# Turning the context rows of six batches and one gated tile by transposing transfers instead of TensorE, in a fused attention and FP4 feed-forward kernel

## The chip, the cores and the metric

The kernel runs on one core of one Trainium2 chip. Its time is the device time of one execution in microseconds (us); several executions give a median. One further execution is recorded by the hardware profiler: its rows give every instruction with start and duration, its "span" runs from the first to the last instruction. The engines are named as the profile names them: PE is TensorE (PEld its weight loads), DVE is VectorE, ACT is ScalarE, POOL is GpSimd and SP is SyncE, which issues all DMA transfers of this kernel. All arithmetic is in 32-bit floats.

## The reference, cut to what matters

There are 8 batches (B) of x, 512 rows (S) of 256 values (D), and for each batch 64 context rows z. For every batch:

```python
y0 = layernorm(x)
r  = layernorm(y0 + softmax(causal(y0 @ y0.T / 16)) @ y0) * g1 + beta1
r  = layernorm(r + softmax(r @ z.T / 16) @ z) * g2 + beta2           # cross attention
r  = layernorm(r + relu(r @ w1 + b1) @ w2 + b2) * g3 + beta3         # MLP, 1024 wide
x  = x + r
q  = fp4(layernorm(x))                                               # blocks of 16 along the row
h  = silu(q @ fp4(w_gate).T) * (q @ fp4(w_up).T)                     # 704 wide
x  = x + fp4(h) @ fp4(w_down).T
```

`fp4` scales each block of 16 by its largest magnitude and rounds to eight magnitudes and a sign. Every product contracts over the last dimension of both operands or over rows, so many tiles are needed transposed, with the contracted dimension on the 128 partitions.

## The kernel before

Each batch is five stages: 0 load and self attention, 1 cross attention, 2 MLP, 3 quantization of the normed x and the gate and up products, 4 quantization of h and the down product. The 512 rows are four tiles of 128 (NT = 4), D is two chunks of 128 (ND = 2). The MLP is 64 products a batch at L985 (512 columns wide, eight hidden chunks) and L1005; the gate and up products stand at L1060, the down product at L1140 (six chunks for each of four tiles).

**Order.** Nothing is issued as the code is read. Every function records operations in a `Plan`: engine, modelled cost, tiles read and written. `Plan._keys` gives each operation a key, the latest start by which it would meet its batch's and stage's entry in the table `DUE`: a due reaches back through all successors, and within a batch from each PE operation to the one before it, so the smallest due of a later stage decides. `push` is added to the keys of the weights' preparation, of fills and of loads. `Plan.order` then plays a list schedule with modelled costs, transfer delays (`lag`) and tile homes: a free engine takes the ready operation with the smallest key, if a home is free for each tile that it first uses. The list that results is emitted once, and each engine and SP's queue follow it strictly in order; semaphores make an instruction wait for its inputs. So `DUE`, the `push` values, and the numbers of homes (`plan.kind`, `plan.share`) set the order, and an instruction that waits holds up all behind it on its engine.

**Two ways to transpose.** `transposed` (L419) lets PE transpose blocks against the identity into a PSUM bank (L427), and ACT copies the bank to SBUF. `turned_by_transfers` (L861) has ACT copy the tile so that the low and the high 16-bit halves of the 32-bit values lie apart (L867), writes it to DRAM (L873), and reads it back by a 16-bit transposing transfer (L878) that lays the halves side by side again. Which way y0, r and r again go is set by `BY_PRODUCTS` (4, 2, 1): PE does it for y0 of the first four batches, for r in cross attention of the first two, and for r in the MLP of the first. The quantized x (`zqT`) always goes by transfers.

**z.** `load` (L351) puts the 64 rows of z twice into a 128-partition tile (`z`, L368), with columns of ones from a fill. `cross_attention` (L884) turns z by PE for every batch: two transposes of 64x128, and ACT writes `zT` with the factor 1/16 (L891). `zT` is the stationary operand of the key products at L907, from which ACT copies `kq` (L920), PE transposes it (L924) and so on to the values product at L951, which reads z itself.

**The down product.** `down` (L1086) quantizes h and makes `hqT`. For all batches but the last: ACT sets the halves apart (L1095), SP writes `hd` (L1101) and issues the transposing transfer (L1106). For the four tiles of the last batch `turned_by_products` (L1116) transposes six blocks on PE, four at L427 and two at L1126, and ACT evicts them in three copies (L1119, L1129, L1130). `last` (L1135) does the product at L1140, the addition to x on DVE (L1151) and the write of the result (L1158). In the last batch all four gate and up tiles are recorded ahead of the four down tiles.

Of the kernel before, what the change touches and what calls it, by code (L numbers as in the profile page):

```python
# [12 lines left out]
U16 = mybir.dt.uint16  # L13
AF = mybir.ActivationFunctionType
# [5 lines left out]
P = 128  # L20
# [18 lines left out]
TURN = 2.6  # L39
# [2 lines left out]

TILED = 2.65

BY_PRODUCTS = (4, 2, 1)
LOAD_EARLY = 2121.0
DUE = [
    [-1946.0, 1210.0, 1271.0, -94.0, 168.0],
    [-339.0, 1223.0, -124.0, -48.0, 115.0],
    [-106.0, 818.0, -121.0, 513.0, 497.0],  # L50
    [2633.0, 342.0, -95.0, 819.0, 286.0],
    [1411.0, 380.0, 1328.0, 1549.0, 28.0],
    [594.0, -260.0, -745.0, -950.0, 427.0],
    [741.0, -2228.0, 778.0, 530.0, 88.0],
    [812.0, 363.0, 145.0, 267.0, -1093.0],
    [-2273.0],
]


# [8 lines left out]
def act(cols, bias=False):  # L68
    return 0.06 + cols * 0.84e-3 + 0.19 * bias
# [193 lines left out]
def kernel(  # L263
# [19 lines left out]
    nc = tc.nc  # L283

    B, S, D = x.shape
    SZ = z.shape[1]
    DFF = w1.shape[1]
    I = w_gate.shape[0]
    NT = S // P
    ND = D // P  # L290
    NF = DFF // P
    NI = -(-I // P)
# [7 lines left out]
    dram = ctx.enter_context(tc.tile_pool(name="dram", bufs=1, space=DRAM))  # L300
# [6 lines left out]
    def several(name, count, shape):  # L307
        return [fixed(f"{name}_{k}", shape) for k in range(count)]


    plan = Plan(due=DUE)
# [1 line left out]

    y0_homes = several("y0", 2, [P, NT, D + 2])

    z_homes = several("z", 8, [P, D + 2])
    plan.kind("y0", y0_homes)
    plan.kind("z", z_homes)
    plan.kind("zT", several("zT", 6, [P, ND, SZ]))
    plan.kind("turned", several("turned", 3, [P, ND, S]), ordered=False)  # L320
    plan.share("y0T", "turned", 3)
    plan.share("yT", "turned", 3, ordered=False)
    plan.share("zqT", "turned", 3)
    plan.kind("e", several("e", 1, [P, NT * (NT + 1) // 2 * P]))
    plan.kind("r", several("r", 3, [P, NT, D]))
    plan.kind("kq", several("kq", 4, [P, S // 2]))
    plan.kind("xp", several("xp", 1, [P, NT, SZ]))
    plan.kind("xpT", several("xpT", 7, [P, NT // 2 * P]))
    plan.kind("hT", several("hT", 9, [P, S]))
    plan.kind("zq", several("zq", 1, [P, NT, D]))  # L330
    plan.kind("zm", several("zm", 2, [P, NT * D]), ordered=False)
    plan.kind("wide", several("h", 8, [P, NI * P]), ordered=False)
    plan.share("h", "wide", 5)
    plan.share("hm", "wide", 4)
    plan.share("wq", "wide", 5)
    hqT_homes = several("hqT", 3, [P, NI * P])
    plan.kind("hqT", hqT_homes)

    hd_homes = [dram.tile([P, 2, NI * P], U16, tag=f"hd_{k}", name=f"hd_{k}") for k in range(3)]
# [3 lines left out]
    zd_homes = [dram.tile([NT, P, 2, D], U16, tag=f"zd_{k}", name=f"zd_{k}") for k in range(4)]  # L343
    plan.kind("zd", zd_homes, ordered=False)
    plan.kind("ln", several("ln", 13, [P, 48]), ordered=False)
    plan.kind("q", several("q", 6, [P, 3, 64]), ordered=False)
    plan.kind("rt", several("rt", 7, [P, 4]), ordered=False)
    banks = [psum.tile([P, 512], F32, tag=f"bank{k}", name=f"bank_{k}") for k in range(8)]
    plan.kind("bank", banks, ordered=False)
# [511 lines left out]
    def turned_by_transfers(v, view, m, yT):  # L861
# [19 lines left out]
            reads=[d], writes=[(yT, c) for c in range(ND)], lag=TURN,  # L881
        )

    def cross_attention(b, r, zs):  # L884

        plan.stage = 1
        zT = plan.buf("zT")
        transposed(
            lambda: [zs.ap[:SZ, ts(c, P)] for c in range(ND)], [(zs, 0)], (zT, None),

            lambda pt: nc.scalar.activation(  # L891
                zT.ap, pt[:, : ND * SZ].rearrange("p (c k) -> p c k", c=ND),
                AF.Copy, scale=1.0 / 16.0,
            ),
            act(ND * SZ), 2,
        )
        yT = turned(r, "yT", b < BY_PRODUCTS[1], lambda t: r.ap[:, t, :])
        sc, nm, xp = plan.buf("bank"), plan.buf("rt"), plan.buf("xp")

        keys = plan.buf("bank")

        def products():
            for c in range(ND):
                for i in range(2):
                    nc.tensor.matmul(  # L907
                        keys.ap[ts(i, SZ), : S // 2], zT.ap[:, c, :], yT.ap[:, c, ts(i, S // 2)],
                        start=(c == 0), stop=(c == ND - 1),
                    )  # L910

        def exps():
            for t in range(NT):
                nc.scalar.activation(
                    xp.ap[:, t, :], sc.ap[:, ts(t, SZ)], AF.Exp, bias=nm.ap[:, t : t + 1]
                )

        plan.op("PE", 1.05, products, reads=[yT, zT], writes=[keys])
        kq = plan.buf("kq")
        plan.op("ACT", act(S // 2), lambda: nc.scalar.copy(kq.ap, keys.ap[:, : S // 2]), reads=[keys], writes=[kq])  # L920

        def scores():
            for j in range(2):
                nc.tensor.transpose(sc.ap[:, ts(j, P)], kq.ap[:, ts(j, P)], ident)  # L924

        plan.op("PE", 0.24, scores, reads=[kq], writes=[sc])
        plan.op(
            "DVE", 0.36,
            lambda: nc.vector.tensor_reduce(
                nm.ap, sc.ap[:, : NT * SZ].rearrange("p (t k) -> p t k", k=SZ),  # L930
                AX.X, ALU.max, negate=True,
            ),
            reads=[sc], writes=[nm],
        )
        plan.op("ACT", 0.8, exps, reads=[sc, nm], writes=[xp], table="exp")
        xpT = plan.buf("xpT")
        transposed(
            lambda: [
                xp.ap[:, 2 * j : 2 * j + 2, :].rearrange("p t k -> p (t k)") for j in range(NT // 2)
            ],  # L940
            [xp], (xpT, None), lambda pt: nc.scalar.copy(xpT.ap, pt[:, : NT // 2 * P]),
            act(NT // 2 * P), NT // 2,
        )
        s = plan.buf("ln")
        avs = [plan.buf("bank") for _ in range(NT)]


        def values():
            for k in range(NT):
                half = ts(k % 2, SZ)  # L950
                nc.tensor.matmul(  # L951
                    avs[k // 2 + NT // 2 * (k % 2)].ap[:, : D + 2], xpT.ap[half, ts(k // 2, P)],
                    zs.ap[half, :],
                    start=True, stop=True,
                )

        plan.op("PE", TILED * pe(D + 2), values, reads=[xpT, zs], writes=avs)
        for t in range(NT):
            av, rt = avs[t], plan.buf("rt")

# [82 lines left out]
    def glu(b, xs, s):  # L1043
# [5 lines left out]
        zT = plan.buf("zqT")  # L1049
# [36 lines left out]
        def down(t, h):  # L1086
            plan.stage = 4
            m = fp4(h, lambda h=h: h.ap[:, :I], "hm", NBI)
            hqT = plan.buf("hqT")
            if b < B - 1:  # L1090
                hd = plan.buf("hd")
                planes = lambda: m.ap[:, :I].bitcast(U16).rearrange("p (h k) -> p h k", h=2)
                plan.op(
# [4 lines left out]
                    reads=[h], writes=[m],  # L1098
# [61 lines left out]
            )  # L1160


        if b == B - 1:
            hs = [gate_up(t) for t in range(NT)]
            for t in range(NT):
                down(t, hs[t])
        else:
            for t in range(NT):
                down(t, gate_up(t))
# [13 lines left out]

    plan.op("PE", 0.22 * WARM, warm, writes=[idle])
    columns()
    plan.push = 3314.0
    plan.op(
        "POOL", 0.2, lambda: nc.gpsimd.memset(nothing, 0), writes=[(ready["fills"], "nothing")]
    )
# [15 lines left out]
        "SP", 5.2, lambda: nc.sync.dma_start(w2_sb, w2.rearrange("(c p) d -> p c d", p=P)),  # L1205
        writes=[ready["w2"]],
    )
    plan.push = 3314.0
    weights()
    plan.push = 0.0  # L1210
    for b in range(B):
# [38 lines left out]
```

## Time and profile before

| what | value |
|---|---|
| median of three runs | 577.25 us (576.84 to 577.31) |
| profiled execution | 577.01 us |
| its span, first to last instruction | 575.1 us |
| mean granted clock of PE | 0.999 |
| PE busy | 567.1 us, 2231 matmuls |
| DVE busy | 447.3 us |
| ACT busy | 361.2 us |
| transfers by the page | 66.88 MB, mean 116 GB/s |
| PE transposes of z (L427) | 16, 2.2 us busy |
| PE transposes of the last batch's h (L427, L1126) | 16 and 8, 2.4 and 2.2 us busy |

Busy time counts the time in which an engine runs at least one instruction; PE's matmuls overlap one another, so a row's mean length is more than the time it takes out of PE's stream, and the distance from one start to the next is what a run of them costs. In answers that list groups, a row has the start and the length in us, then engine, line, operation, output from input, the count, and in brackets how long the engine had been idle and what released it. In the chain of waits, each piece is the part of the time that one group accounts for on the path to the end.

### The profile page before, as it was taken

How to read it: one execution, taken by the hardware profiler on the slowest of the kernel's cores; microseconds unless marked ns; L12 is line 12 of the kernel's file. 1: busy time of each engine (PE TensorE's matmuls, PEld its weight loads, DVE VectorE, ACT ScalarE, POOL GpSimd, SP SyncE). 2: the span in 40 equal slices, each digit the busy share in tenths (PEclk: the TensorE clock that was granted, in tenths of full speed). 3: DMA queues.
4: the chain of work that ended last, by engine and by line, in shares of the span. 5: the costliest groups of instructions: out<-in, count | busy, mean ns of one | idle time of the engine just before them, and what ended most of it. 6: DMA issues, size and time to landing. Idle time of an engine off the chain costs nothing.

```text
span 575.1 us, 7092 instructions
## 1 busy us (share of the span) xinstructions
PE 567.1 (99%) x2231; PEld 395.7 (69%) x2231; DVE 447.3 (78%) x1128; ACT 361.2 (63%) x758; POOL 63.7 (11%) x93
## 2 busy tenths in 40 slices
PE   8999999999999999999999999999999999999997
PEld 6757584775577668476686666767674867877686
DVE  5889968989397964679479999989898457489892
ACT  2678858697967674676727457959766255455331
POOL 3421101011101200200100001200010000000000
PEclk9999999999999999999999999999999999999999
DMA  8550395273737044054422646893455221645601
GB/s 243 126 192 7 91 228 137 69 203 63 177 99 185 11 90 97 24 133 99 118 46 73 162 124 153 206 200 80 118 158 137 62 62 38 161 108 150 161 18 46
DMA packets 143220, 66.88 MB, mean 116 GB/s; under 512 B 107976, under 2 KB 142672, under 8 KB 143184
## 3 DMA queue, kind: packets, MB, share of 16 engines
q1 hardware_dynamic: 143184, 66.44, 45.3%
q8 instruction: 17, 0.28, 0.2%
q14 instruction: 19, 0.16, 0.1%
HBM read 10.42 MB, written 29.66 MB: 70 GB/s over the span
## 4 chain that ended last, share of the span: by engine, by line
PE 94%; DVE 2%; DMA 1%; ACT 1%; POOL 1%; issue 0%; SPq 0%
PE bank L1060 25%; PE bank L1005 19%; PE bank L985 19%; PE bank L1140 14%; PE bank L818 6%; PE bank L785 5%; PE bank L427 2%; PE bank L951 1%; PE bank L907 1%; DMA turned<-zd 1%; POOL ln L511 1%; DMA x<-in_x_dram 0%; DVE x L574 0%; DVE r L825 0%; ACT squares L496 0%
## 5 line engine op out<-in xcount | busy, mean ns | idle before, releaser
L1060 PE MATMUL bank<-wgu,turned 128*128 128x352 f32 x512 | 157.7, 461 | 0.0
L1060 PEld LDWEIGHTS bank<-wgu,turned 128*128 128x128 f32 x512 | 96.4, 190 | 52.6 <-issue 3.9
L1005 PE MATMUL bank<-w,hT 128*128 128x256 f32 x512 | 113.5, 380 | 0.0
L985 PE MATMUL bank<-turned,w 128*128 128x512 f32 x256 | 112.9, 594 | 0.4 <-DMA turned<-zd 0.4
L1005 PEld LDWEIGHTS bank<-w,hT 128*128 128x128 f32 x512 | 96.8, 190 | 14.1 <-issue 0.4
L985 PEld LDWEIGHTS bank<-turned,w 128*128 128x128 f32 x256 | 48.2, 190 | 56.3 <-issue 50.4
L1140 PE MATMUL bank<-wd,hqT 128*128 128x256 f32 x384 | 86.4, 380 | 0.0
L1140 PEld LDWEIGHTS bank<-wd,hqT 128*128 128x128 f32 x384 | 72.8, 190 | 12.9 <-issue 2.0
L511 POOL TENSOR_TENSOR ln<-ln,mhalf 128x4 f32<-128x4 f32 x32 | 40.4, 1262 | 355.1 <-DVE ln L504 355.1
L620 DVE SCALAR_TENSOR_TENSOR h<-h,h 128x704 f32<-128x704 f32 (+2 forms) x76 | 66.8, 883 | 7.9 <-ACT h L614 7.6
L496 ACT ACTIVATE squares<-r,ln 128x256 f32<-128x256 f32 x96 | 48.7, 507 | 26.7 <-DVE ln L488 24.4
L993 ACT ACTIVATE hT<-bank,cols 128x512 f32<-128x512 f32 x64 | 42.9, 683 | 24.3 <-PE bank L985 24.1
L1072 ACT ACTIVATE h<-bank 128x352 f32<-128x352 f32 x64 | 29.0, 460 | 42.5 <-PE bank L1060 42.2
L1095 ACT COPY h<-h 128x1408 uint16<-128x1408 uint16 x28 | 38.0, 1363 | 19.3 <-DVE h L627 14.9
L614 ACT ACTIVATE h<-h 128x704 f32<-128x704 f32 (+2 forms) x38 | 29.8, 787 | 21.1 <-DVE h L608 16.6
L1079 DVE TENSOR_TENSOR h<-h,bank 128x352 f32<-128x352 f32 x64 | 32.3, 510 | 11.6 <-PE bank L1060 5.2
L785 PE MATMUL bank<-turned 128*128 128x512 f32 (+3 forms) x128 | 38.3, 444 | 0.3 <-ACT turned L853 0.2
L818 PE MATMUL bank<-y,e 128*128 128x258 f32 x160 | 37.0, 383 | 0.4 <-POOL e L805 0.4
L595 DVE TENSOR_REDUCE q<-h 128x44 f32<-128x704 f32 (+2 forms) x38 | 33.2, 878 | 2.9 <-DMA h<-in_L_ffn_w_up_dram 2.8
L818 PEld LDWEIGHTS bank<-y,e 128*128 128x128 f32 x160 | 30.1, 190 | 6.6 <-issue 1.0
L1016 DVE SCALAR_TENSOR_TENSOR r<-bank,r 128x256 f32<-128x256 f32 x32 | 13.4, 421 | 26.9 <-PE bank L1005 26.6
L608 DVE SCALAR_TENSOR_TENSOR h<-h,q 128x704 f32<-128x704 f32 (+2 forms) x38 | 33.4, 884 | 0.2
(94 smaller groups left out, 645.1 us busy)
## 6 DMA issues: line engine op xcount, KB each, us to landing
zd<-zm SPq DMA_DIRECT2D x25, 512.0 KB, 3.1
hd<-h SPq DMA_DIRECT2D x30, 352.0 KB, 3.1
out_dram<-x SPq DMA_DIRECT2D x32, 128.0 KB, 1.7
x<-in_x_dram SPq DMA_DIRECT2D x7, 512.0 KB, 4.9
w<-in_L_xattn_w_dram SPq DMA_DIRECT2D x2, 1024.0 KB, 6.4
z<-in_ctx_dram SPq DMA_DIRECT2D x16, 64.0 KB, 5.2
zd<-h SPq DMA_DIRECT2D x2, 384.0 KB, 4.7
h<-in_L_ffn_w_down_dram SPq DMA_DIRECT2D x2, 352.0 KB, 3.8
```

Of the source, the lines that this page charges most:

```text
L496: lambda t=t: nc.scalar.activation(squares, view(t), AF.Square, bias=s.ap[:, 24 + t : 25 + t], accum_out=s.ap[:, 28 + t : 29 + t],),
L511: lambda: nc.gpsimd.tensor_tensor(s.ap[:, 36:40], s.ap[:, 32:36], mhalf, ALU.pow),
L608: lambda: nc.vector.scalar_tensor_tensor(blocks_of(view()), blocks_of(view()), TIE, each(rc()), ALU.mult, ALU.mult),
L620: lambda reverse=reverse, f=f: nc.vector.scalar_tensor_tensor(view(), mm(), LEAST, view(), ALU.max, f, reverse1=reverse),
L785: nc.tensor.matmul(sc.ap[:, :n], yT.ap[:, c, ts(k, P)], yT.ap[:, c, k * P :], start=(c == 0), stop=(c == ND - 1),)
L818: nc.tensor.matmul(av.ap[:, : D + 2], e.ap[:, ds(start[k] + (t - k) * P, P)], y0.ap[:, k, :], start=(k == 0), stop=(k == t),)
L985: nc.tensor.matmul(hp.ap, w1_sb[:, c, ts(f, P)], yT.ap[:, c, :], start=(c == 0), stop=(c == ND - 1),)
L993: lambda f=f, hp=hp, h=h: nc.scalar.activation(h.ap, hp.ap, AF.Relu, bias=b1_sb[:, f : f + 1]),
L1005: nc.tensor.matmul(fp.ap[:, :D], hT[f].ap[:, ts(t, P)], w2_sb[:, f, :], start=(f == 0), stop=(f == NF - 1),)
L1060: nc.tensor.matmul(gp.ap[:, :HI], zT.ap[:, c, ts(t, P)], wgu[:, c, ds(j * I + n * HI, HI)], start=(c == 0), stop=(c == ND - 1),)
L1095: lambda: nc.scalar.copy(planes(), h.ap[:, :I].bitcast(U16).rearrange("p (k h) -> p h k", h=2)),
L1140: nc.tensor.matmul(op.ap[:, :D], hqT.ap[:, ts(c, P)], wd[:, c, :], start=(c == 0), stop=(c == NI - 1),)
```

## The change

z of batches 0 and 1 is still turned by PE; from batch 2 on the new function `z_by_transfers` does it: a scaled copy of the 64 rows on ACT, a second ACT copy that sets the halves apart, a write to DRAM and a transposing transfer into `zT`, both issued by SP. The last batch's first tile of h (t = 0) goes the way of the other batches' tiles; its other three still go by PE. Homes are added for the new tiles (`zzd` in DRAM, `zpl` in SBUF), and several numbers of homes, the dues, and the pushes of loads, fills and weights are other numbers.

```diff
+Z_BY_PRODUCTS = 2
 BY_PRODUCTS = (4, 2, 1)
-LOAD_EARLY = 2121.0
+LOAD_EARLY = 2211.0
 DUE = [
-    [-1946.0, 1210.0, 1271.0, -94.0, 168.0],
-    [-339.0, 1223.0, -124.0, -48.0, 115.0],
-    [-106.0, 818.0, -121.0, 513.0, 497.0],
-    [2633.0, 342.0, -95.0, 819.0, 286.0],
-    [1411.0, 380.0, 1328.0, 1549.0, 28.0],
-    [594.0, -260.0, -745.0, -950.0, 427.0],
-    [741.0, -2228.0, 778.0, 530.0, 88.0],
-    [812.0, 363.0, 145.0, 267.0, -1093.0],
-    [-2273.0],
+    [-2135.0, 912.0, 1321.0, -107.0, 321.0],
+    [-352.0, 741.0, 238.0, -35.0, 165.0],
+    [164.0, 846.0, -113.0, 420.0, 733.0],
+    [3239.0, 169.0, -88.0, 878.0, 398.0],
+    [879.0, 335.0, 1676.0, 1843.0, 36.0],
+    [598.0, -989.0, -910.0, -604.0, 416.0],
+    [263.0, -2512.0, -326.0, 906.0, -708.0],
+    [-1000.0, -823.0, -1514.0, -1037.0, -2102.0],
+    [-2343.0],
 ]
...
-    z_homes = several("z", 8, [P, D + 2])
+    z_homes = several("z", 7, [P, D + 2])
...
-    plan.share("y0T", "turned", 3)
+    plan.share("y0T", "turned", 1)
...
-    plan.kind("kq", several("kq", 4, [P, S // 2]))
-    plan.kind("xp", several("xp", 1, [P, NT, SZ]))
-    plan.kind("xpT", several("xpT", 7, [P, NT // 2 * P]))
-    plan.kind("hT", several("hT", 9, [P, S]))
+    plan.kind("zzd", [dram.tile([SZ, 2, D], U16, tag=f"zzd_{k}", name=f"zzd_{k}") for k in range(4)])
+    plan.kind("zpl", several("zpl", 4, [SZ, D]))
+    plan.kind("kq", several("kq", 2, [P, S // 2]))
+    plan.kind("xp", several("xp", 3, [P, NT, SZ]))
+    plan.kind("xpT", several("xpT", 8, [P, NT // 2 * P]))
+    plan.kind("hT", several("hT", 8, [P, S]))
...
-    plan.share("hm", "wide", 4)
-    plan.share("wq", "wide", 5)
-    hqT_homes = several("hqT", 3, [P, NI * P])
+    plan.share("hm", "wide", 8)
+    plan.share("wq", "wide", 7)
+    hqT_homes = several("hqT", 4, [P, NI * P])
...
-    plan.kind("q", several("q", 6, [P, 3, 64]), ordered=False)
+    plan.kind("q", several("q", 11, [P, 3, 64]), ordered=False)
...
+    def z_by_transfers(zs, zT):
+        zpl, zd = plan.buf("zpl"), plan.buf("zzd")
+        def apart():
+            nc.scalar.mul(zpl.ap, zs.ap[:SZ, :D], 1.0 / 16.0)
+            nc.scalar.copy(
+                zpl2.ap.bitcast(U16).rearrange("p (h k) -> p h k", h=2),
+                zpl.ap.bitcast(U16).rearrange("p (k h) -> p h k", h=2),
+            )
+        zpl2 = plan.buf("zpl")
+        plan.op("ACT", act(D) + act(2 * D), apart, reads=[(zs, 0)], writes=[zpl, zpl2])
+        plan.op(
+            "SP", 0.5,
+            lambda: nc.sync.dma_start(
+                zd.ap, zpl2.ap.bitcast(U16).rearrange("p (h k) -> p h k", h=2)
+            ),
+            reads=[zpl2], writes=[zd], takes=[zT], lag=1.5,
+        )
+        plan.op(
+            "SP", 0.6,
+            lambda: nc.sync.dma_start_transpose(
+                zT.ap.rearrange("p c k -> p (c k)").bitcast(U16).rearrange(
+                    "p (c r) -> p c r", c=ND
+                ),
+                zd.ap.rearrange("p h k -> (p h) k"),
+            ),
+            reads=[zd], writes=[zT], lag=TURN,
+        )
...
-        transposed(
...
+        if b < Z_BY_PRODUCTS:
+            transposed(
...
+        else:
+            z_by_transfers(zs, zT)
...
-            if b < B - 1:
+            if b < B - 1 or t < 1:
...
-    plan.push = 3314.0
+    plan.push = 4718.0
...
-    plan.push = 3314.0
+    plan.push = 4718.0
```

More of the change, by code (lines that the diff above doesn't have):

```diff
@@ L887, in cross_attention @@
         zT = plan.buf("zT")
-        transposed(
[L889 to L896, printed above, removed]
+        if b < Z_BY_PRODUCTS:
+            transposed(
+                lambda: [zs.ap[:SZ, ts(c, P)] for c in range(ND)], [(zs, 0)], (zT, None),
+                lambda pt: nc.scalar.activation(
+                    zT.ap, pt[:, : ND * SZ].rearrange("p (c k) -> p c k", c=ND),
+                    AF.Copy, scale=1.0 / 16.0,
+                ),
+                act(ND * SZ), 2,
+            )
+        else:
+            z_by_transfers(zs, zT)
         yT = turned(r, "yT", b < BY_PRODUCTS[1], lambda t: r.ap[:, t, :])
```

## The prediction

> **What bounds the kernel now.** I read first the page's busy times, then the table of busy time by stretch, then TensorE (PE) alone in order of time, then the chain that ended last, and at the end the DMA issues. The page:
>
> ```profile
> span 575.1 us, 7092 instructions
> ...
> PE 567.1 (99%) x2231; PEld 395.7 (69%) x2231; DVE 447.3 (78%) x1128; ACT 361.2 (63%) x758; POOL 63.7 (11%) x93
> ```
>
> PE is busy 567.1 of 575.1 us. The profiled execution took 577.01 us, 1.91 us of it outside the span; the median of the three runs is 577.25 us, 0.24 us more. I sum against 577.01. Where the 8.0 idle us lie is told by the stretches (columns: stretch, its length, busy us of each engine, granted clock, DMA share, GB/s):
>
> ```profile
> 0.00:45.00 45.00, 40.89 (x197) 29.40 (x198) 33.79 (x140) 25.34 (x67) 15.91 (x40) 1.00 0.62 179
> 45.00:130.00 85.00, 85.00 (x334) 57.73 (x334) 74.07 (x204) 67.42 (x155) 11.30 (x16) 1.00 0.50 126
> 130.00:300.00 170.00, 169.56 (x645) 114.67 (x644) 120.74 (x317) 113.55 (x247) 16.51 (x18) 1.00 0.39 95
> 300.00:440.00 140.00, 139.68 (x531) 95.38 (x531) 129.78 (x297) 97.74 (x180) 15.66 (x16) 1.00 0.58 146
> 440.00:550.00 110.00, 110.00 (x420) 79.63 (x419) 76.03 (x151) 51.83 (x96) 4.36 (x4) 1.00 0.37 97
> 550.00:575.10 25.10, 21.98 (x112) 18.89 (x110) 12.91 (x24) 5.36 (x15) 0.00 (x0) 0.98 0.11 37
> ```
>
> The reader is to see that from 45 to 550 us PE is idle for 0.44 + 0.32 = 0.76 us in all; 4.11 us are lost before 45 and 3.12 us after 550, nearly all of the latter behind the last matmul. So a PE instruction taken out after 45 us is worth what it occupies, as long as other engines keep feeding. Before 45 us it is worth that only where PE wasn't about to wait anyway.
>
> **Part 1: z of batches 2 to 7.** Two 64-wide transposes for each of six batches go, twelve in all. In the old kernel every z is turned early, before it is needed (L427 in order of time):
>
> ```profile
> 14.69 0.46 PE L427 MATMUL bank<-ident,z 64*128 64x64 f32 x4
> ...
> 32.42 0.34 PE L427 MATMUL bank<-ident,z 64*128 64x64 f32 x2
> ...
> 33.70 0.59 PE L427 MATMUL bank<-ident,z 64*128 64x64 f32 x6
> 35.33 0.44 PE L924 MATMUL bank<-ident,kq 128*128 128x128 f32 x2 [1.05 <-ACT kq L920]
> ...
> 44.04 0.34 PE L427 MATMUL bank<-ident,z 64*128 64x64 f32 x2
> ```
>
> z tiles are taken in order of batch. The first pair (at 6.30 us) is batch 0; the four at 14.69 are batches 1 and 2, then 3, then 4 to 6, then 7. The chain of waits gives the four at 14.69 a share of 0.39 us and the last pair 0.27 us; so one costs about 0.10 to 0.13 us there. On the chain are therefore batch 2's pair, 0.20, and batch 7's, 0.27: **0.47 us**. The eight of batches 3 to 6 lie beside DVE and POOL work, at 8 x 0.105 = 0.84 us; the six at 33.70 are followed by a PE wait of 1.05 us for ACT, so with the order unchanged their removal only lengthens waits. The new order may put other work there: 0 to 0.84 us. I take 0.4, the middle, since the transposes of batch 3's y stand 16 us later in the same list (49.61) and need only a load and a norm.
>
> What replaces them: per batch two ACT instructions, two transfers. ACT: the first is a 64x256 scaled copy, bounded by the 128x256 eviction at L920, 367 ns, and the 128x256 ACT write of y at L541, 595 ns; the second has the form of L867 (512 uint16 columns), 615 ns on 128 rows. Gone is L891, 268 ns. Net 0.71 to 0.94 us a batch, 4.3 to 5.7 us in all, on an engine with 214 us idle. ACT is fullest between 45 and 130 us (67.4 of 85), and 17.6 us are free even there; nothing on the chain, and some 0.9 us for an ACT-fed matmul if the cover is gone.
>
> SP: a write to DRAM and a transpose for each batch. Not in this trace; the nearest rows in both directions:
>
> ```profile
> hqT<-hd SPq DMA_TRANSPOSE x28, 4.0
> turned<-zd SPq DMA_TRANSPOSE x25, 4.3
> ...
> rest_d<-h SPq DMA_DIRECT2D x2, 64.0 KB, 2.8
> ...
> wgu<-rest_d SPq DMA_TRANSPOSE x4, 2.3
> ```
>
> The write is near rest_d (2.8 us to landing); the transpose of 128 x 256 lies between wgu<-rest_d (2.3) and turned<-zd (4.3). Chain of z: 1.0 + 2.8 + 2.3 to 4.3 + the copies' handovers = about 6 to 8.5 us. Consumers are the eight groups of L907: batch 2 at 88.0, then 160.1, 170.9, 220.1, 386.4 and 404.0. z has landed by about 32 us, so 50 us or more cover it; cost nothing, and up to 8.5 us once if the planner issued a z right before its L907. On SP, issue is 0.34 to 0.63 us for the write and 1.1 to 1.4 us for the transpose: 9 to 12 us more in 575 on a queue whose waits already add to hundreds of us. Behind each new wait (the write for ACT, the transpose for the write) stand the yT and hqT transfers; PE's one wait on such a transfer today is 0.44 us (L985 for turned), so I charge 0 and keep 0.4 us for each that meets a tight one.
>
> The trace has PE turn a z block in about 0.1 us of its stream and a transfer land in 2.3 us at best. The Trainium skill, page "VectorE: DVE Perf Modes", section "The three transpose paths", speaks against the change: 390 ns by TensorE against 1309 ns by DMA for 128x128, and its rules prefer TensorE where PSUM will do. If every block were waited for, an estimate from that page is 12 x 0.92 = 11 us lost. The trace decides otherwise: latency hides behind a full PE, and this kernel pays in PE time.
>
> **Part 2: the last batch's first gated tile.** Four 128-wide transposes at L427 and two at L1126 go. The chain at the end:
>
> ```profile
> 551.15 5.18 PE bank L1140 x24
> 556.33 0.44 PE bank L427 x4
> 556.77 0.22 PE bank L1126 x2
> 556.99 0.44 PE bank L427 x4
> 557.42 0.22 PE bank L1126 x2
> 557.64 7.77 PE bank L1140 x36
> ```
>
> One tile is 0.44 + 0.22 = **0.66 us**, all on the chain. Its replacement: h is final at 546.02 (DVE L627 at 545.19 for 0.83); ACT copy L1095 1.36 us; then as batch 6's last tile did it, the write issued at 539.15 and the transpose at 542.40, 3.25 us, and 4.0 us to landing (5.7 at most). 546.0 + 0.2 + 1.4 + 3.3 + 4.0 = 554.9, worst 556.6. Its products are due after three tiles of batch 6: 551.0 + 3 x 2.59 = 558.8. Cover of 2 to 4 us; without it (its products drawn ahead of batch 6's) PE would wait up to about 4 us. ACT loses evictions of 0.59 + 0.27 + 0.28 and gains 1.36: nothing. Next late is tile 3: h final at 562.1, while PE is occupied to 565.4; pulling PE forward by 1.5 us leaves 1.8. The 3.1 us behind the last matmul stay.
>
> **Part 3: homes and dues.** No work is added, but the planner's order changes everywhere. z 8 to 7, hT 9 to 8, kq 4 to 2 tighten; xp, hqT, q, hm widen. A due reaches backwards through a batch's PE chain, so the smallest due behind a stage counts: batch 1's middle goes from -124 to -35, behind batch 3; batch 6's later stages from 88 to -708; the weights' push from 3314 to 4718 and most `down` dues up. GLU of the early batches is thus deferred somewhat. The bounds by rows: it can win at most the 0.76 us in the middle and about 1.9 us of the head (the gaps between 7.6 and 45 us: 37.4 less 35.5); it can lose what DVE lacks, below. I take 0.
>
> **Sum:** 0.47 + 0.4 + 0.66 = 1.53; 577.01 - 1.53 = 575.48, say **575.5 us**.
>
> **The rivals.** (a) *Gaps refilled too*: all 12 + 6 transposes count (0.47 + 0.84 + 0.66 = 1.97) and the new order also takes 1 to 2.6 of the idle 0.76 + 1.9: 574.0 to 572.4. For it: the waits before 45 us are short and many; against: batch 0's norms (DVE and POOL, 31 to 39 us) fix PE's start. (b) *Traded for new waits*: only the sure 1.13 is won and 0.4 to 1.5 us of new waits appear, as PE met one 0.44 us wait for a transfer and one 0.32 for ACT: 576.3 to 577.4. That the change doesn't do what it says belongs here: if z's transposes were only cover, 0.66 alone remains, 576.35. (c) *Slower, DVE becomes the bound of the GLU stretch*: between 300 and 440 us DVE is busy 129.8 of 140, and 10.2 us is all it has left. One gated tile costs DVE five passes of about 0.88, 0.61 for the scales, two products of 0.51 and an add of 0.42: 6.4 us. Deferring up to one tile from before 300 (where 49 us are idle) into that stretch costs nothing; from the second on PE waits: two tiles 12.8 - 10.2 = 2.6, two and a half 5.8. Against 1.53 won: 578.1 at two, 581.3 at two and a half; it decides for slower from 10.2 + 2.9 = 13.1 us of DVE work moved there. For it: dues of `down` rise for batches 0 to 3; against: in the last 110 us before the tail DVE has 34 us free, so the work can move there. The trace shows the clock at 1.00 through gaps up to 1.05 us. The skill's "TensorE: Matmul & The Clock Gate", section "Why this matters for your kernels", warns of PE gaps over about 3 us; no run here shows one in mid-kernel.
>
> **How the numbers follow.** About 0.2% (1.15 us) is what a measurement of this kernel can tell from no change: the boundaries are 576.1 and 578.4. Forecast (574.3 to 576.1) 0.42; (a) 0.20; (b) 0.24; (c) 0.14, nearly all above 578.4. Faster 0.62, same 0.25, slower 0.13. The range 572.8 to 578.8 holds the forecast, nearly all of (a), (b) and the light end of (c); about 0.15 are outside.
>
> **What would show it.** Right: L427 with z has 4 instead of 16 instructions, those with h 12, L1126 6; PE's busy time falls by 1.5 to 2 us; 45 to 550 us stays within 1 us of full. Wrong: a PE wait at L907 for a transfer of zT (part 1's cover), at L1140 for hqT near the end (part 2's), or idle PE beside a DVE above 95% (c). If PE's busy time falls so and the span doesn't, the head's waits took it.

## The result, and the profile after

The changed kernel takes 579.1 us in the median of 19 runs (577.07 to 581.22), the kernel before 576.86 us in 19 runs beside it (576.54 to 577.74): a ratio of 1.0035, 95% interval 1.0025 to 1.0045. The prediction, 575.5 us and faster, was wrong: the kernel is 2.2 us slower, above the upper end of the range too.

Six of the 19 runs held a mean TensorE clock of 0.999 or 1.0 and took 577.07 to 578.39 us; the other thirteen had 0.996 or 0.997 and took 578.16 to 581.22. The profiled execution, 577.07 us, is the fastest of all. It shows what was lost at full clock; the rest has to be sought in another execution (experiment 1).

The page of the changed kernel:

```profile
span 575.4 us, 7063 instructions
...
PE 563.7 (98%) x2213; PEld 392.1 (68%) x2213; DVE 447.3 (78%) x1128; ACT 365.9 (64%) x762; POOL 67.4 (12%) x93
```

There are 18 matmuls fewer, as foreseen, and PE's busy time fell by 3.4 us (567.1 to 563.7). But the span grew from 575.1 to 575.4. So PE's idle time rose from 8.0 to 11.7 us, 3.7 us more than before. The same stretches as before tell where (columns as in the prediction):

```profile
0.00:45.00 45.00, 38.97 (x190) 28.24 (x191) 34.34 (x146) 28.82 (x72) 16.83 (x41) 1.00 0.63 169
45.00:130.00 85.00, 84.84 (x324) 55.55 (x323) 75.50 (x204) 70.23 (x161) 13.88 (x16) 1.00 0.61 149
...
300.00:440.00 140.00, 138.21 (x518) 92.71 (x517) 127.73 (x293) 98.30 (x182) 15.50 (x15) 1.00 0.59 144
...
550.00:575.40 25.40, 21.71 (x110) 18.91 (x108) 6.85 (x14) 3.12 (x10) 0.00 (x0) 1.00 0.35 92
```

Idle PE time is length less busy time: before 45 us it grew from 4.11 to 6.03, between 45 and 130 from 0 to 0.16, between 300 and 440 from 0.32 to 1.79, behind 550 from 3.12 to 3.69; between 130 and 300 it fell from 0.44 to 0, and from 440 to 550 it stayed at 0. The sum of these is 1.92 + 0.16 + 1.47 + 0.57 - 0.44 = 3.68. PE's waits put names to the two large ones (columns: who waited for whom, us in total, times, longest):

```profile
PE bank L944 <- DMA turned<-zd: 1.8, 1, 1.8
PE bank L821 <- POOL e L808: 1.6, 1, 1.6
PE bank L961 <- ACT kq L957: 1.5, 1, 1.5
```

L944 is the key product (L907 before), L821 the self attention's values (L818), L961 kq's turning (L924). In the kernel before, these three products waited 0.3, 0.4 and 1.05 us:

```profile
PE bank L924 <- ACT kq L920: 1.0, 1, 1.0
...
PE bank L818 <- POOL e L805: 0.4, 1, 0.4
PE bank L907 <- ACT h L614: 0.3, 1, 0.3
```

The first of the three, at 386.89 us, is batch 6 waiting for its turned r; the others lie at 25.83 and 35.05 us, in the head. The values product is set by POOL in both kernels: it starts at 26.11 us before and at 25.83 after, and PE only comes to it earlier.

The chain at the end carries three tiles' transposes instead of four; between the 48 matmuls and the 36 there is one pair of pieces of 0.44 and 0.22 us, where before there were two:

```profile
543.84 10.36 PE bank L1177 x48
...
554.86 7.77 PE bank L1177 x36
```

No PE wait stands there for the tile that goes by transfers.

### The profile page after: what moved, and what is told of

Same layout as the page of the kernel before. It is cut to its first block, busy times and chain, and to the rows that moved or that the text cites. A ratio compares the mean times of both kernels' runs of the same rounds, so it can differ in the third digit from the quotient of the medians.

```text
span 575.4 us, 7063 instructions
## 1 busy us (share of the span) xinstructions
PE 563.7 (98%) x2213; PEld 392.1 (68%) x2213; DVE 447.3 (78%) x1128; ACT 365.9 (64%) x762; POOL 67.4 (12%) x93
## 4 chain that ended last, share of the span: by engine, by line
PE 91%; DMA 2%; DVE 2%; SPq 2%; ACT 1%; issue 1%; POOL 0%; DVEq 0%
PE bank L1097 26%; PE bank L1042 19%; PE bank L1022 19%; PE bank L1177 14%; PE bank L821 5%; PE bank L788 4%; PE bank L988 1%; DMA x<-in_x_dram 1%; PE bank L944 1%; PE bank L430 1%; DMA turned<-zd 1%; DVE ln L459 1%; ACT squares L499 0%; ACT turned L856 0%; SPq L363 0%
## 5 line engine op out<-in xcount | busy, mean ns | idle before, releaser
L1097 PE MATMUL bank<-wgu,turned 128*128 128x352 f32 x512 | 158.0, 460 | 0.0
L1097 PEld LDWEIGHTS bank<-wgu,turned 128*128 128x128 f32 x512 | 96.0, 190 | 52.7 <-issue 3.6
L1132 ACT COPY h<-h 128x1408 uint16<-128x1408 uint16 x29 | 39.3, 1361 | 20.4 <-DVE h L630 14.5
L1030 ACT ACTIVATE hT<-bank,cols 128x512 f32<-128x512 f32 x64 | 42.8, 682 | 11.8 <-PE bank L1022 11.7
L821 PE MATMUL bank<-y,e 128*128 128x258 f32 x160 | 37.3, 384 | 1.6 <-POOL e L808 1.6
L821 PEld LDWEIGHTS bank<-y,e 128*128 128x128 f32 x160 | 29.9, 190 | 8.2 <-POOL e L808 1.8
L630 DVE TENSOR_TENSOR h<-h,q 128x704 f32<-128x704 f32 (+2 forms) x38 | 33.3, 884 | 0.1
```

Source lines behind the costliest of these rows:

```text
L821: nc.tensor.matmul(av.ap[:, : D + 2], e.ap[:, ds(start[k] + (t - k) * P, P)], y0.ap[:, k, :], start=(k == 0), stop=(k == t),)
L1030: lambda f=f, hp=hp, h=h: nc.scalar.activation(h.ap, hp.ap, AF.Relu, bias=b1_sb[:, f : f + 1]),
L1097: nc.tensor.matmul(gp.ap[:, :HI], zT.ap[:, c, ts(t, P)], wgu[:, c, ds(j * I + n * HI, HI)], start=(c == 0), stop=(c == ND - 1),)
L1132: lambda: nc.scalar.copy(planes(), h.ap[:, :I].bitcast(U16).rearrange("p (k h) -> p h k", h=2)),
```

## The experiments

The theories in short: **clock** (z's transposes kept PE busy early; without them its waits grow, and after longer waits the granted clock drops), **copies** (ACT's new copies delay kq), **queue** (the new transfers hold up others on SP) and **dues** (the new order loses by itself). Each experiment is compared with the kernel before on the same chip, since the latter's medians were 577.11, 576.93 and 577.16 us beside experiments 1 to 11 and 575.71 beside the last two. Nothing of the computation is left out in any experiment; the filling transposes and the spare copies write results that nothing uses.

### 1. The changed kernel again

Edit: none.

> The changed kernel unaltered, to get a profile of an execution at the lower clock that most of its executions show (0.996 to 0.997). Order theory (the new order lets PE wait for a late transfer, most of all the transposed r of batch 6 ahead of the key products, and the clock is then lowered for a stretch): a profile of about 578 to 580 us has one PE gap of 3 us or more in mid-kernel, and right behind it a stretch of a few us at a clock well under 1. Edit theory (the added transfers and ACT copies cost by themselves): the loss is spread, with no gap over 2 us.

Measured: 580.52 us against 577.11, ratio 1.0051 (1.0031 to 1.0071). The profiled execution took 580.72 us at a mean clock of 0.997, so this execution lost clock. Its table by stretches of 2 us, of PE alone (busy time, granted clock, DMA share, GB/s):

```profile
34.00:36.00 2.00, 0.59 (x3) 1.00 1.07 346
36.00:38.00 2.00, 2.00 (x3) 0.52 0.32 113
38.00:40.00 2.00, 2.00 (x6) 0.63 0.00 0
```

and PE in order of time:

```profile
26.13 2.88 PE L821 MATMUL bank<-y,e 128*128 128x258 f32 x12 [2.27 <-POOL e L808]
...
35.36 0.44 PE L961 MATMUL bank<-ident,kq 128*128 128x128 f32 x2 [1.50 <-ACT kq L957]
35.84 3.60 PE L788 MATMUL bank<-turned 128*128 128x512 f32 x4
```

The same products in the first profile, at full clock:

```profile
25.83 2.88 PE L821 MATMUL bank<-y,e 128*128 128x258 f32 x12 [1.61 <-POOL e L808]
...
35.54 1.98 PE L788 MATMUL bank<-turned 128*128 128x512 f32 x4
```

PE was idle for 2.27 us, ten us later for 1.50 us, and then the clock fell to 0.50 for 3.4 us (36.1 to 39.5, which the two stretches of 2 us above catch in part): four matmuls that take 1.98 us in the first profile take 3.60 here. Set beside the first profile, instruction by instruction, this execution is 0.30 us late at 26 us and 1.87 us late at 37.4; so 1.57 of the final 3.65 us arise in these 11 us. Another 0.96 come at 132 us (from 2.65 to 3.61 late), where L1097 waits 0.80 us, and the rest in pieces of a few tenths.

### 2 and 3. The old order with both edits, and with z alone

Here the order of the kernel before is kept word for word. z of batches 2 to 7 is copied apart by ACT where ACT evicted `zT` before, and SP issues the twelve transfers together (in experiment 3 from 63.1 to 74.6 us); experiment 2 also has the tile by transfers. Experiment 3's edit takes out the two PE transposes and puts the copies where ACT's eviction was:

```diff
+        if b >= 2:
+            plan.ops[-2].emit = lambda: None
+            plan.ops[-1].emit = lambda: z_by_transfers(b, zs, zT)
```

> The old kernel's order word for word, with both edits put into it by hand: z of batches 2 to 7 by transfers, their writes and transposes issued together where SP is idle at about 61 us, and the last batch's first gated tile by transfers. Order theory: 0.6 to 1.2 us faster than before (576.86 less 1.13 of PE time on the chain, about 575.7 to 576.3). Edit theory: 1 us or more slower than before, with the clock below 0.999.

> The old order with z by transfers alone. Order theory: 0 to 0.5 us faster (0.47 of the twelve transposes lay on the chain). Edit theory: slower by 0.5 us or more.

Measured: 580.22 us, ratio 1.0058 (1.0038 to 1.0079) with both edits, and 580.54 us, ratio 1.0059 (1.0043 to 1.0075) with z alone; every execution of both lies at a clock of 0.993 to 0.997. ACT ahead of kq, in experiment 3:

```profile
34.20 0.40 ACT L889 ACTIVATE zpl<-z 64x256 f32<-64x256 f32 x1
34.63 0.62 ACT L890 COPY zpl<-zpl 64x512 uint16<-64x512 uint16 x1
...
36.26 0.36 ACT L946 COPY kq<-bank 128x256 f32<-128x256 f32 x1
```

and PE behind it:

```profile
36.67 0.69 PE L950 MATMUL bank<-ident,kq 128*128 128x128 f32 x2 [3.55 <-ACT kq L946]
37.15 3.35 PE L788 MATMUL bank<-turned 128*128 128x512 f32 x4
```

Two such pairs of copies (the second at 35.28; 2 x 1.02 us) take the place of two evictions (0.42 us together), and nothing fills PE meanwhile: its wait grows from 1.05 to 3.55 us, and the clock falls to 0.63 and 0.52 in the four us from 36 on. So the old order loses as much with z by transfers as the new one. It doesn't lose it in the same way: in the changed kernel's first profile two pairs of copies run from 26.98 to 29.0 us, and none stands between them and kq's copy at 34.65 us.

### 4. The old order with the tile alone

The tile's PE transposes and evictions go, and behind the last step of its h stand one ACT copy, a write and a transpose into a home of its own:

```diff
+                    def by_transfers():
+                        of_h()
...
+                        nc.scalar.copy(
+                            planes, h.ap[:, :I].bitcast(U16).rearrange("p (k h) -> p h k", h=2)
+                        )
+                        nc.sync.dma_start(hd[:, :, :I], planes)
+                        nc.sync.dma_start_transpose(
...
```

> The old order with the last batch's first gated tile by transfers alone. Order theory: 0.66 us faster, as six PE transposes at the end go and the transfer has 2 to 4 us of cover. Edit theory, or the cover being gone: PE waits at the down product near 558 us and the time is unchanged or up to 4 us slower.

Measured: 575.88 us against 577.11, ratio 0.9978 (0.9968 to 0.9989). This is the one arrangement that is faster than the kernel before, by 0.6 to 1.8 us, and its executions hold a clock of 0.999 or 1.0. The transfer is issued long before PE needs it:

```profile
550.53 1.40 SPq L1131 DMA_TRANSPOSE hqT_extra<-hd  x1
```

It lands 3.7 us later, at 554.3; the tile's products begin at 559.75. Against the profile of before, this execution is 0.34 us late at 386.8 us and 0.32 us early behind the tile, at 557.2: 0.66 us from the tile, as predicted.

One more row is to be kept, as it returns below. The execution is 0.87 us ahead of the profile of before from 12 to 123 us, and at 132 us only 0.39 us of that is left:

```profile
132.14 4.10 PE L987 MATMUL bank<-turned,w 128*128 128x512 f32 x9 [0.92 <-DMA turned<-zd]
```

In the kernel before this product (L985) waited 0.44 us. The transfer left 0.82 us earlier too (127.18 against 128.00), but took 4.82 us to land instead of 4.39.

### 5. The old kernel with ACT's copies only

No transfer and no PE edit: all z are transposed by PE as before, and two spare pairs of copies stand ahead of batch 0's kq.

```diff
+        if b in (5, 6):
+            of_zT = plan.ops[-1].emit
+            def more():
+                of_zT()
+                nc.scalar.mul(spare[0], zs.ap[:SZ, :D], 1.0 / 16.0)
+                nc.scalar.copy(
...
```

> The old kernel, all z still turned by TensorE and no transfer added; only two scratch copy pairs of the z size on ACT (results unused) ahead of batch 0's copy kq, where the old order with z by transfers had its own. Clock theory (what costs is a PE gap of some 2 to 3.5 us between 32 and 37 us, and the lower clock that follows it, not the transfers): a PE wait for kq of 2.5 to 3.2 us, a stretch of about 3.5 us at half clock behind it in most executions, 1.5 to 3.5 us slower than before. Transfer theory (the added DMA and SP work costs): within 0.8 us of before.

Measured: 580.92 us against 576.93, ratio 1.0066 (1.0052 to 1.008), all clocks 0.993 to 0.997. PE's wait for kq and the stretch with it:

```profile
PE bank L937 <- ACT kq L933: 3.0, 1, 3.0
```

```profile
30.00:40.00 10.00, 7.03 (x39) 0.77 0.77 262
```

From 40 to 50 us the clock is 0.89; in finer slices it is 0.50 from 35.4 to 42.3 us. Neither transposing transfers nor missing transposes are needed for a loss of this size: a PE wait of 3 us in this place is enough. Of the 4.0 us, 1.9 are the longer wait (2.97 less 1.05) and most of the rest is the clock: the same four matmuls take 3.78 us instead of 1.98.

### 6 and 7. The old order, z's copies and transfers later; and filled

Experiment 6 moves the copies of five batches to 74 to 84 us and their transfers to about 106 to 122. Experiment 7 adds the tile by transfers, and lets PE transpose the identity where it had turned z of batches 3 to 6:

```diff
-FILLED = ()
+FILLED = (3, 4, 5, 6)
...
+    def pe_fill(bank):
+        for c in range(2):
+            nc.tensor.transpose(bank[:, ts(c, SZ)], ident[:SZ, :], ident[:SZ, :SZ])
```

> The old order with z by transfers, but the ACT copies of batches 3 to 7 put between 74 and 84 us and their transfers near 108 us, so that nothing new stands ahead of kq; the PE transposes of z are simply gone. Clock theory: the wait for kq is about 1.5 to 2.2 us (1.05 and the time of the z transposes that went); if that is still short enough the clock holds and the time is 0 to 0.5 us better than before, if not it is 1 to 2 us worse in part of the executions. Transfer theory: 2 to 3.5 us worse in all, as with the early copies.

> The old order with both edits, ACT copies late as in the run before, and eight transposes of the identity (results unused) where those of z of batches 3 to 6 stood. Clock theory: PE has the old gaps, the clock holds, and the time is 1.0 to 1.7 us better than before (0.66 to 1.2 from the tile, 0.2 to 0.5 from z of batches 2 and 7), the best of all. Transfer theory: 1 to 2 us worse than before.

Measured: 583.36 us, ratio 1.0112 (1.0089 to 1.0136), and 582.87 us, ratio 1.0109 (1.0094 to 1.0124). Both missed. The head was mended, in experiment 7 fully: kq waits 0.7 us, the clock stays at 1.00 from 30 to 40 us, and PE runs up to 1.37 us ahead of before until 130 us. Then, in experiment 7 (4.9 us in experiment 6):

```profile
PE bank L1025 <- DMA turned<-zd: 4.7, 1, 4.7
```

SP's queue ahead of it, in experiment 7:

```profile
112.95 4.12 SPq L906 DMA_TRANSPOSE zT<-zzd  x3
...
119.39 2.54 SPq L906 DMA_TRANSPOSE zT<-zzd  x2
...
130.60 1.64 SPq L886 DMA_TRANSPOSE turned<-zd  x1
```

and the last of these in the kernel before:

```profile
128.00 1.73 SPq L878 DMA_TRANSPOSE turned<-zd  x1
```

The five transposes of z lie where each turned tile's write, landing and transpose follow one another: the second and third turned tiles leave SP 2.75 and 2.60 us later than before (125.14 against 122.39, 130.60 against 128.00). PE, which came early, waits for the third; behind the wait of 4.70 us the clock is 0.91 over the 20 us from 130 on.

### 8. The changed kernel with filled gaps

```diff
+                if b == 1 and t == 0:
+                    for _ in range(14):
+                        nc.tensor.transpose(av.ap[:, :P], ident, ident)
...
+            if b == 0:
+                for _ in range(10):
+                    nc.tensor.transpose(sc.ap[:, :P], ident, ident)
```

The order of the changed kernel, with 14 transposes of the identity ahead of the values product that waited 1.6 us and 10 ahead of kq's turning.

> The changed kernel with 14 and 10 transposes of the identity (results unused) ahead of the two early PE waits, the values product of batch 1 and the turning of kq of batch 0. Clock theory: the clock holds in nearly every execution, the median falls from 579.1 to 580.5 to 577.3 to 578.3, where the undisturbed-clock executions of the changed kernel lie. Transfer theory: no change, 579 to 580.5.

Measured: 578.77 us against 576.93, ratio 1.0029 (1.0019 to 1.0039); all nine executions hold 0.998 to 1.0. The two waits shrink:

```profile
PE bank L824 <- POOL e L808: 0.9, 1, 0.9
```

The other, kq's, is 0.3 us. So the clock can be held by work of no use. Whether time is won with it isn't settled (1.0029 against 1.0051 in experiment 1 and 1.0035 in the first measurement, with overlapping intervals); and 1.8 us of loss remain at a full clock.

### 9 and 10. The new dues and homes without the edits

Experiment 9 lets PE turn z of all batches in the changed kernel, experiment 10 also the tile; the planner makes its order anew from the new table.

```diff
-Z_BY_PRODUCTS = 2
+Z_BY_PRODUCTS = 8
...
-            if b < B - 1 or t < 1:
+            if b < B - 1:
```

> The changed kernel with its dues, homes and the tile by transfers, but z of all batches by TensorE again (the planner's order is made anew with those twelve transposes in it). Clock theory: z's early transposes stand again where PE would wait, the clock holds, and the time is 576.0 to 577.8: at or under the old kernel. If the new dues themselves cost (late transfers near 130 and 387 us): 577.5 to 579 at an undisturbed clock. Transfer theory of z: 576 to 577.

> The changed kernel's dues and homes alone: z and the last batch's first tile by TensorE as in the old kernel. Clock theory with harmless dues: 576.5 to 578, some 0.5 to 1.2 us above the run with the tile by transfers. If the dues cost: 578 to 580, again 0.5 to 1.2 above that run.

Measured: 580.0 us, ratio 1.005 (1.0037 to 1.0063), and 580.18 us, ratio 1.0063 (1.0041 to 1.0086), against 577.16. Dues and homes alone lose as much as the whole change. They do so at full clock too: three of experiment 9's five executions and four of experiment 10's six hold 1.0, and these lie 1.9 to 2.8 and 2.1 to 3.4 us above the kernel before. The two profiled executions are among those that lost clock. In them the values product L821 waits 2.0 and 2.3 us for POOL (in two waits each, the longer ones 1.8 and 2.1), kq's turning 1.4 us, and the down product 1.3 and 1.7 us for hqT. This table was not made for an order with z on PE, so the two parts can't be added up; it shows that part 3 is not free.

### 11. The old order, both edits, filled and spread

As experiment 7, but the copies of batches 2, 3, 4 and 7 stay where the evictions were, their transfers go at 61 us, and the transposes of batches 5 and 6 go behind the last turned tile.

```diff
+AT_ACT = {5: 76.5, 6: 81.5}
+AT_SP = {
+    2: (61.0, 63.5), 3: (61.2, 63.7), 4: (61.4, 63.9), 7: (61.6, 64.1),
+    5: (108.0, 136.0), 6: (108.7, 136.5),
+}
```

> The old order with both edits, eight identity transposes in place of those of batches 3 to 6, the ACT copies of batches 5 and 6 moved to about 80 us, and the transfers where SP is idle: four at 61 us, the writes of batches 5 and 6 near 108, their transposes near 134 us. Clock theory: no wait for kq beyond the old one, no late transposed r at 132 us, clock near 1: 575.0 to 576.0, as good as the tile alone or up to 0.5 better. If 578 or more, then z's transfers cost even when kept away from gaps and tight queue entries.

Measured: 580.06 us, ratio 1.004 (1.0026 to 1.0053); missed. Three of the eight executions held a clock of 0.999 or 1.0 and took 578.2 to 578.45 us, so the loss is not the clock's alone; the other five took 580.03 to 580.72. The wait for kq is 0.7 us and PE is 1.2 us ahead of before until 132.5; then it waits 2.06 us for the same turned tile. That tile's transpose is issued at 127.42, 0.6 us earlier than before, but takes 5.35 us to land instead of 4.39. Its issue alone took 2.84 us instead of 1.73, and z's two transposes were issued only at 131.82, behind it; what slowed it isn't shown.

### 12 and 13. A home more, and experiment 8 once more

In the changed kernel SP's queue stood still from 31 to 41 us, waiting for a free z home (the number of homes went from 8 to 7):

```profile
40.99 1.14 SPq L371 DMA_DIRECT2D z<-in_ctx_dram  x2
...
47.41 0.58 SPq L657 DMA_DIRECT2D h<-in_L_ffn_w_gate_dram  x1
```

Experiment 12 is experiment 8 with its order unchanged and a home of its own for batch 7's z; experiment 13 is experiment 8 unaltered.

```diff
+    z_more = fixed("z_more", [P, D + 2])
+    of_z(z_more)
...
+    z_bufs[7].home = z_more
```

> The changed kernel's order and the fillers of e8, and batch 7's z gets a home of its own (an eighth), so that SP's queue does not stand from 31 to 41 us for a free z. Theory of the queue (part of the remaining 1.8 us at full clock is SP's standstill, after which all loads and the transfers near 130 us are late): the load of w_gate is issued some 10 us earlier, no PE wait of 0.8 at 132 us, 0.5 to 1.5 us less than e8, 577.3 to 578.2. Rival (the remaining loss lies elsewhere, in the late transfer of batch 6's turned tile at 387 us and the end): as e8, 578.4 to 579.1.

> e8 unaltered, beside e12 on one chip, to see where its remaining 1.8 us lie in an execution that is not its fastest. Theory of the queue: PE waits at 132 us for a turned tile, which e12 does not have. Rival: the waits are the same in both, at 387 us and behind the last product. Time 577.2 to 579.4.

Measured on one chip, with 575.71 us for the kernel before: 576.59 us, ratio 1.0005 (0.999 to 1.002), with the home; 577.05 us, ratio 1.0025 (1.0013 to 1.0037), without. SP in experiment 12:

```profile
31.24 1.23 SPq L374 DMA_DIRECT2D z_more<-in_ctx_dram  x2
...
46.44 0.58 SPq L662 DMA_DIRECT2D h<-in_L_ffn_w_gate_dram  x1
```

The z load goes 10 us earlier, as expected; the load of `w_gate` only 1.6 us earlier than in experiment 13 (48.07), since SP now waits for other things in between, and neither has the wait of 0.8 us at 132. The medians differ by 0.46 us and the intervals overlap a little, so a gain from the home is likely, and its size isn't settled. Both keep a PE wait of about 1 us at 386 us (1.05 and 0.94), where the kernel before has 0.3.

## Why the prediction was wrong

**What was right.** Part 2: the tile's 0.66 us is real, as experiment 4's rows show; its medians differ by 0.6 to 1.8 us. h's transfer landed 5.5 us ahead of its use. DVE work did not move into the stretch from 300 to 440 us (DVE is busy 127.73 there, 129.78 before), so rival (c)'s mechanism did not happen, though its time did. The sign given for the work was not met: PE's busy time fell by 3.4 us where 1.5 to 2 was named. Busy time is a poor measure of so little work: experiment 4, with six transposes fewer, has 564.9 us, 2.2 less than before.

**The step that failed first** put the transfers at nothing: "PE's one wait on such a transfer today is 0.44 us (L985 for turned), so I charge 0". With it fails the reading of the table by stretches, that a PE instruction taken out is worth what it occupies unless PE idles; it was read from PE's idle time alone. The kernel before has two places where a transfer sets PE's start, at 132.52 and at 386.44 us. At the second, the view puts the wait of 0.32 us down to ACT, and the prediction took it so ("one 0.32 for ACT"). But r's transpose, issued at 382.02, landed at 386.30, and the product started 0.14 us behind that landing, just as at the first place (132.39 and 132.52) and in the changed kernel (386.76 and 386.89). The kernel before:

```profile
377.14 0.57 SPq L873 DMA_DIRECT2D zd<-zm  x1
...
382.02 2.07 SPq L878 DMA_TRANSPOSE turned<-zd  x1
```

```profile
386.44 1.08 PE L907 MATMUL bank<-turned,zT 128*64 128x256 f32 x8 [0.32 <-ACT h L614]
```

The changed kernel:

```profile
376.80 0.74 SPq L876 DMA_DIRECT2D zd<-zm  x1
...
382.19 2.43 SPq L881 DMA_TRANSPOSE turned<-zd  x1
```

```profile
386.89 1.08 PE L944 MATMUL bank<-turned,zT 128*64 128x256 f32 x8 [1.79 <-DMA turned<-zd]
```

The chains of both kernels have the same groups ahead of this place, and the changed kernel's PE is 1.01 us ahead in them (373.65 against 374.66). The write of r leaves SP only 0.34 us earlier and lands 0.18 us later (382.13 against 381.95); its transpose leaves 0.17 us later and lands 0.46 us later. So PE waits 1.79 us and goes on 0.45 us late. All that it had won by then is lost: 1.47 us of new waiting, where 0 was charged and 0.4 kept in mind. How much of the 1.01 us was z's isn't shown, since the wait at 132 us is gone in this order too.

At the first place SP's queue sets the time. In the kernel before:

```profile
113.87 0.39 SPq L873 DMA_DIRECT2D zd<-zm  x1
116.86 2.13 SPq L878 DMA_TRANSPOSE turned<-zd  x1
119.05 0.58 SPq L873 DMA_DIRECT2D zd<-zm  x1
122.39 2.02 SPq L878 DMA_TRANSPOSE turned<-zd  x1
124.50 0.53 SPq L873 DMA_DIRECT2D zd<-zm  x1
...
128.00 1.73 SPq L878 DMA_TRANSPOSE turned<-zd  x1
```

and the chain of waits behind it:

```profile
128.00 4.39 DMA turned<-zd
...
132.52 5.39 PE bank L985 x12
```

Three writes and three transposes follow one another, each transpose issued within 0.1 us of the landing of its write, 18.5 us from the first write to the last landing. In experiment 4 the first write came 0.87 us earlier, as PE did, but the six took 19.0 us; they took 19.9 us in experiment 11, and 22.8 us in experiment 7 with z's transposes among them. PE was 0.87, 1.2 and 1.37 us ahead of before there, and behind the wait it was 0.39 ahead, 0.38 late and 2.89 late. A gain ahead of such a place counts as far as the transfers come earlier too. All of z's transposes lie ahead of both places; those of the last tile lie behind both and count.

**Part 1's cover was looked at from the wrong side.** The text asked who waits for the new transfers of z, and nobody does: no profile here shows a PE wait for `zT`. (The "2.3 us at best" named for a landing holds for transposing transfers; the writes of the result land in 1.7 us.) It did not ask what z's old transposes did for PE. Its 0.47 us for batches 2 and 7 was right as far as 44 us: in the old order experiments 6, 7 and 11 gained 0.50 to 0.54 us on the kernel before between 12 and 44 us. The eight others won nothing there: their work of 0.59 us at 33.70 us stood beside a wait of 1.05 us, and experiment 6, without them, gained as much as experiment 7, where fills stood in their place. The text said so ("only lengthens waits") and then took 0.4 us for a refill by the new order. No refill shows: idle time before 45 us grew by 1.92 us, more than the 1.3 to 1.6 that twelve transposes take at 0.105 to 0.13. And the longer waits were not free, since they can cost clock. Two more terms were mis-sized in the old order: ACT's "some 0.9 us for an ACT-fed matmul if the cover is gone" was 2.5 us in experiment 3 (3.55 less 1.05), since two pairs of copies met one eviction, and SP's 0.4 us for each transfer that meets a tight one was up to 4.3 us in experiment 7 (4.70 less 0.44).

**The clock** stood in the prediction as one sentence without a price. The skill's rule, in the Trainium skill, "TensorE: Matmul & The Clock Gate", section "Why this matters for your kernels", speaks of gaps over about 3 us. Waits of 3.55 and 2.97 us in experiments 3 and 5 agree with it. Experiment 1's did not need that much: 2.27 us and, ten us later, 1.50 us were followed by half the clock, while 1.61 and 1.49 us in the first profile of the same kernel were not. The measurement decides: the changed kernel sits at the edge, and thirteen of its nineteen executions fall over it. The median of those is 579.62 us, of the six others 577.9: 1.7 us between the two sorts, near the 1.62 us by which the four matmuls are longer in experiment 1.

**Part 3, taken at 0,** had bounds by idle PE time and by DVE. The new table and homes lose 3 us with z and the tile both on PE (experiment 10). PE's long waits in that profile are for POOL, ACT and a transfer, so DVE, which was named as the bound, isn't it. SP's standstill for a z home is one piece, likely. "z 8 to 7 ... tighten" was in the text, without the question which queue would wait for the missing home.

**Where the loss lies, then.** In the fastest execution, the profiled one, PE loses at 386.89 us what it had won and then wins the tile: its last addition starts 0.26 us earlier than before (571.75 against 572.01). The span is longer all the same, as the time behind that start grew from 3.1 to 3.6 us, for a reason that isn't located. The six executions at full clock are about 1.0 us slower than before (577.9 against 576.86); the 0.8 us by which their median lies above the profiled one are not located either. Experiments 8 and 13, filled, lie 1.8 and 1.3 us above the kernel before. With the clock lost it is 1.7 us more. Rival (b), gains traded for new waits, had the mechanism, but only at 0.4 to 1.5 us and without the clock. Open remain the share of each due, what the longer waits owe to z's going and what to the new order, and what keeps experiment 12 from the gain of the tile that experiment 4 has; the wait of about 1 us at 386 us is the only one that its profile shows to be longer than before behind 130 us.

## What to carry to other kernels

An instruction that comes off a full engine counts only as far as the later points at which that engine waits for somebody else come earlier too: look for such waits, even of 0.3 or 0.4 us, before counting gains ahead of them, and compare the landing of a transfer with the start behind it, as the name that a view gives for a wait can be the wrong one. Ask of removed work not only who needs its result but which gap it filled, and of each added copy or transfer what stands behind it in its queue. The tile alone, behind the last such wait and with 5.5 us of cover, is the version to keep: 0.9978 (0.9968 to 0.9989).

## What the runs showed of the hardware

**The length of a lost clock.** Read in slices of 0.25 us, the granted clock is 0.50 for about 3.4 us in experiments 1 (36.1 to 39.5 us), 2, 3, 6, 7, 9 and 11, for 3.4 us twice in experiment 10, and for 6.8 us in experiment 5; on both sides it is 1.00.

**Where it begins.** That isn't tied to the end of the wait: it begins 0.7 us behind it in experiment 1, 0.1 to 0.2 us ahead of it in experiments 2 and 3, and 1.2 us ahead of it in experiment 5, while PE still waits.

**How long a wait has to be** isn't one number here. Waits of 1.37 us (experiment 10), 1.81 us (experiment 9), 2.06 us (experiment 11) and 2.14 us (experiment 10) were followed by half the clock. Waits of 1.61 and 1.79 us (the first profile of the changed kernel) and 1.75 us (experiment 10) were not, and the 2.27 us in experiment 1 was not until the next wait came ten us later. Every wait of 2.97 us and more was (experiments 2, 3, 5, 6 and 7). The changed kernel fell to either side.

**What holds it.** With 24 transposes of the identity in the two gaps, the mean clock was 0.998 to 1.0 in all 29 executions of experiments 8, 12 and 13; without them 17 of 25 executions of the changed kernel had 0.996 or 0.997.
